# Attention stage of a grid-LSTM, attention and feed-forward kernel: the place of one transposition, and the shape of one product

## The chip, the cores and the metric

The kernel runs on one core of a Trainium2 chip. The metric is the time of one execution on the device in microseconds (us), as the median of several runs. The engines are TensorE (PE, with its weight loads shown apart as PEld), VectorE (DVE), ScalarE (ACT), GpSimd (POOL) and SyncE (SP, which here issues DMAs). Each has its own queue of instructions and works it off in the order in which the kernel was written; they wait for one another by semaphores.

## The reference

The input x is 16 images of 64 x 64 cells with 128 channels, float32. Three layers follow each other:

```
x = x + grid_lstm(group_norm(x))             # 16 x 64 x 64 x 128
t = tokens(x)                                # 16 x 4096 x 128
n = layer_norm(t)
t = t + n + nystrom_attention(layer_norm(n)) # 8 heads of 16, 64 landmarks, plus a convolution of v over 33 rows
n = layer_norm(t)
t = t + sigmoid_recurrence(batch_norm(n @ W.T))
```

The change is in the attention. With q, k, v the projections of the normalised rows, q_l and k_l the means over 64 rows each (landmarks), it computes softmax(q k_l') pinv(softmax(q_l k_l')) (softmax(q_l k') v) + conv(v), multiplies by w_out, and adds. The last part of the attention stage also makes the next layer's input: the layer norm of the sum, turned, and its product with W ("feed"), which is written to memory for the recurrence.

## The kernel before

The attention stage cuts each image into Q = 8 groups of 512 rows. A group passes through three stages that are an image (8 steps) apart, and several groups are in flight. The Python function `step(s)` writes the instructions of one step; it is used for s = 15 to 127, with `first_step` and `second_step` ahead of it and `last_step` behind. In one step, `new` (group s) is projected to keys, values and queries; `mid` (group s - 8) has its weights softmax(q_l k') formed and multiplied with v; and the groups around s - 16 end: `first` is compared with the landmarks and softened (the exponents of the next step's `attend`), `cur` is attended, convolved and divided, `third` goes through w_out and is added to the stream, `fourth` is measured, `fifth` is normalised (tile z), turned, and fed through W. `after` is group s + 1: its rows (tile xh, loaded two steps before) are turned by four transposes of TensorE so that the next step can project them. Nothing is rearranged by a scheduler: the order in the queues of PE, DVE, ACT and POOL is the order of the calls in `step`.

PSUM has eight banks of 512 float32 columns, used by name: `bank0` to `bank5`, and a `pair` of two. A tile in a bank may only be written when all readers of the tile before it in that bank are done. The uses that matter here, in one step, in order:

- bank 0: keys, then the first of four score tiles of `greatest` (L1028), reduced on DVE by `keep_greatest` (L1032) in the order 3, 2, 1, 0; then the first tile of `soften` (L1170, L1172), read by ACT in `softened` (L1177).
- bank 1: values, a tile of `greatest`, the turned stream of `turn_output` (L960, tile z, copied by ACT to zT, L975), a tile of `soften`.
- bank 2: a tile of `greatest`, the turned maxima of `turn_top` (L1159, copied by ACT to topT, L1163), the reciprocals r of `divide` (L1195, read on DVE in L1197), a tile of `soften`.
- bank 3: a tile of `greatest`, the product with w_out (L1212, read on DVE in `keep_sum`, L1216), the feed (L1244, copied by ACT to fx, L1248), a tile of `soften`.
- banks 4 and 5: `weigh`, then the two tiles of `attend` (L1184), transposed on DVE in `divide` (L1193, tile t); then bank 4 takes the turned rows of `turn_rows` (L960, tile xh, copied by ACT to xT, L968), and bank 5 takes `attend_values` (L1080).
- the pair: `weigh`, then `convolve` (L1107), then `compare` (L1135).

TensorE's order in a step is: `compare`, keys, values, queries (L979), `greatest`, `weigh` (L1058, L1064), w_out, `turn_top`, `turn_output`, `attend`, `convolve`, feed, `turn_rows`, `attend_values`, `soften`. The array can be used whole (128*128) or in tiles; keys, values and queries are written as four tiles of 128 rows by 32 columns by the helper `product(..., apart)` (except in the first step of an image), `attend` and `convolve` use 64*32, `weigh`, `soften` and `compare` use 32*128, and w_out, the transposes and the feed use the whole array. A float32 product appears in the trace as two matmuls, a transpose as one.

ACT's order around the change is: four exponentials of `weights` (L1073), zT, topT, fx, xT, a part of `carry` (L948), the four exponentials of `softened`, another `carry`, keys (L987), values (L997).

Of the kernel before, what the change touches and what calls it, by code (L numbers as in the profile page):

```python
# [845 lines left out]
def attention(nc, tc, t1, gamma, beta, wqkv, ident, mhalf, fixed, xp, rows, qm, km, pinvT, vd, t2, wx, wx_stats, out, ahead):  # L846
# [20 lines left out]
    with ExitStack() as ctx:  # L867
# [10 lines left out]
        def banks(*ks):  # L878
            return [bank(k, [P, GC]) for k in ks]
# [4 lines left out]
        bands, wo, bo, wfT, ones, ones_b, minus, ident_b, split, tops, gs = fixed  # L884
# [71 lines left out]
        def turn(a, k):  # L956

            p = bank(k, [P, C, P])
            for c in range(C):
                nc.tensor.transpose(p[:, c, :], a[:, c, :], ident)  # L960
            return p.rearrange("p c n -> p (c n)")

        def turn_rows(gr, k=4):
            gr.px = turn(gr.xh, k)

        def keep_rows(gr):
            gr.xT = wk.tile([P, GC], F32, tag="xT", name="at_xT", bufs=2)
            nc.scalar.activation(gr.xT, gr.px, AF.Identity, bias=beta, scale=gamma)  # L968
# [4 lines left out]
        def keep_output(gr):  # L973
            gr.zT = wk.tile([P, GC], F32, tag="zT", name="at_zT")
            nc.scalar.copy(gr.zT, gr.pz)  # L975

        def product(out, lhsT, rhs, apart):
            for r in map(quarter, range(NP)) if apart else (slice(0, P),):
                nc.tensor.matmul(out[r], lhsT[:, r], rhs, start=True, stop=True)  # L979

        def project_keys(gr, p=None, apart=False):
            gr.pk = banks(0)[0] if p is None else p
            product(gr.pk, wqkv[:, P : 2 * P], gr.xT, apart)

        def keep_keys(gr):
            gr.KT = kv.tile([P, GC], F32, tag="KT", name="at_KT")
            nc.scalar.copy(gr.KT, gr.pk)  # L987

        def project_values(gr, p=None, apart=False):
            gr.pv = banks(1)[0] if p is None else p  # L990
            for c in range(C):
                cs = slice(c * P, (c + 1) * P)
                product(gr.pv[:, cs], gr.xT[:, cs], wqkv[:, 2 * P : 3 * P], apart)
# [7 lines left out]
        def project_queries(gr, apart=False):  # L1001
            (gr.pq,) = banks(5)
            product(gr.pq, wqkv[:, 0:P], gr.xT, apart)
# [44 lines left out]
        def sums(im):  # L1048
            im.sums = sm.tile([P, P], F32, tag="sums", name="at_sums")
            im.total = wk.tile([P, NP, P], F32, tag="total", name="at_total", bufs=2)  # L1050
# [24 lines left out]
        def attend_values(gr, k=5):  # L1075

            p = bank(k, [P, P])
            for c in range(C):
                for n in range(NP):
                    nc.tensor.matmul(  # L1080
                        p[quarter(n)], gr.V[:, c, quarter(n)], gr.e[:, n, c, :],
                        start=(c == 0), stop=(c == C - 1), skip_group_check=True,
                    )
            gr.p = p

        def keep_values(gr):
            im, p = gr.im, gr.p
            if gr.g == 0:
                nc.vector.tensor_copy(im.sums, p)
            else:  # L1090
                nc.vector.tensor_tensor(im.sums, p, im.sums, ALU.add)
# [37 lines left out]
        def compare(gr):  # L1129

            gr.both = pair()
            gr.s = (*banks(4, 5), gr.both[:, 0], gr.both[:, 1])
            for c in range(C):
                for n in range(NP):
                    nc.tensor.matmul(  # L1135
                        gr.s[n][:, c * P : (c + 1) * P], gr.QT[quarter(n), c * P : (c + 1) * P],
                        gr.im.km[quarter(n)], start=True, stop=True,
                    )

        def topmost(gr):  # L1140
            gr.mx = sm.tile([P, NP, C, 2], F32, tag="cmx", name="at_cmx")
            for s, n, k in ((gr.s[1], 1, 1), (gr.both.rearrange("p n x -> p (n x)"), 2, 2), (gr.s[0], 0, 1)):
                nc.vector.tensor_reduce(  # L1143
                    gr.mx[:, n : n + k].rearrange("p n c j -> p (n c j)"), s.rearrange("p (x m) -> p x m", m=M), AX.X, ALU.max
                )
# [28 lines left out]
        def softened(gr):  # L1174
            gr.eT = wk.tile([P, NP, GC], F32, tag="eT", name="at_eT")
            for n in range(NP):
                nc.scalar.activation(gr.eT[:, n], gr.s[n], AF.Exp)  # L1177
# [42 lines left out]
        def measure(gr, cs=range(C)):  # L1220
            if 0 in cs:
                gr.mu = sm.tile([P, C, 2], F32, tag="mu", name="at_mu")
            for c in cs:
                st = sm.tile([P, 6], F32, tag="st", name="at_st")
                nc.vector.bn_stats(st, gr.u[:, c, :])
                nc.vector.bn_aggr(gr.mu[:, c, :], st)
# [12 lines left out]
                    gr.z[:, c, :], gr.u[:, c, :], AF.Identity, bias=gr.nb[:, c : c + 1], scale=gr.r3[:, c : c + 1]  # L1239
                )  # L1240

        def feed(gr, k=3):
            (gr.pf,) = banks(k)
            nc.tensor.matmul(gr.pf, wfT, gr.zT, start=True, stop=True)  # L1244

        def keep_feed(gr):
            gr.fx = fx = wk.tile([P, GC], F32, tag="fx", name="at_fx")
# [3 lines left out]
        def measure_feed(gr):  # L1251
            nc.vector.bn_stats(wx_stats[:, gr.im.b * Q + gr.g, :], gr.fx)
# [3 lines left out]
        def group(s):  # L1256
            b, g = divmod(s, Q)
            return images[b].groups[g] if b in images else None
# [141 lines left out]
        def step(s):  # L1400
            b, q = divmod(s, Q)
            new, after, mid, was = group(s), group(s + 1), group(s - Q), group(s - Q - 1)
            first, cur, third, fourth, fifth, sixth = (group(s - 2 * Q + d) for d in (1, 0, -1, -2, -3, -4))
            start = q == 0
            if first:
                compare(first)
            if cur:
                softened(cur)
            project_keys(new, apart=not start)
            if start:  # L1410
                sums(mid.im)
            project_values(new, apart=not start)
            if s == 2 * Q - 1:
                attend_values(was, 3)
                keep_values(was)
            if first:
                topmost(first)
            if sixth:
                measure_feed(sixth)
            if fourth:  # L1420
                measure(fourth, (0,))
            keep_keys(new)
            keep_projected(new)
            project_queries(new, apart=not start)
            if start and was:
                gather(was.im)
            if fourth:
                measure(fourth, (1,))
            keep_queries(new)
            if start:  # L1430
                turn_split(mid.im)
            if fifth:
                normalise(fifth)
            greatest(new)
            if first:
                carry_factors(first)
                carry(first, 2, nc.gpsimd)
            weigh(mid)
            keep_greatest(new)
            if first:  # L1440
                part_top(first)
            if third:
                output(third)
            weights(mid)
            if first:
                carry(first, 3, nc.gpsimd)
            if start and was:
                spread_values(was.im)
            if first:
                turn_top(first)  # L1450
            if fifth:
                turn_output(fifth)
                keep_output(fifth)
            if third:
                keep_sum(third)
            if fourth:
                measure(fourth, (2, 3))
            if cur:
                attend(cur)
            if first:  # L1460
                keep_top(first)
            add_weights(mid, (3, 1, 0), mid.g == 0)
            if fourth:
                factors(fourth)
            add_weights(mid, (2,))
            if q == Q - 1:
                shift(new.im)
            if cur:
                convolve(cur, pair())
                divide(cur)  # L1470
            if fifth:
                feed(fifth)
            if after:
                turn_rows(after)
            if fifth:
                keep_feed(fifth)
            if after:
                keep_rows(after)
            if first:
                carry(first, 0, nc.scalar)  # L1480
            attend_values(mid)
            if cur:
                add_convolved(cur)
            keep_values(mid)
            if first:
                soften(first)
                carry(first, 1, nc.scalar)
                carry_bias(first)
            if cur:
                turn_attended(cur)  # L1490
            fetch(s)
# [345 lines left out]
```

## Time and profile before

| what | value |
|---|---|
| median of 3 runs | 3635.04 us (3631.91 to 3635.63) |
| the profiled execution | 3638.43 us, span 3636.9 us |
| PE busy in the span | 3499.9 us (96%) |
| DVE, ACT, POOL busy | 2982.8 (82%), 2499.9 (69%), 2489.2 (68%) |
| mean granted TensorE clock | 0.99 |
| first and last `attend` in `step` | 1734.5 and 3121.2 us |

How to read it: a row of a timeline has the start in us from the start of the span, the duration from there to the end of the last of its instructions, the engine, the line of the kernel, the operation, its output and input tiles, the shape, and the number of instructions. Rows of matmuls overlap: a matmul's record lasts until its last result has left the array, while the next one is already streaming, so the time that a group holds the array is read from its start to the start of the next group. In brackets at the end of a row is the time for which the engine stood idle before it and what it is taken to have waited for.

### The profile page before, as it was taken

How to read it: one execution, taken by the hardware profiler on the slowest of the kernel's cores; microseconds unless marked ns; L12 is line 12 of the kernel's file. 1: busy time of each engine (PE TensorE's matmuls, PEld its weight loads, DVE VectorE, ACT ScalarE, POOL GpSimd, SP SyncE). 2: the span in 40 equal slices, each digit the busy share in tenths (PEclk: the TensorE clock that was granted, in tenths of full speed). 3: DMA queues.
4: the chain of work that ended last, by engine and by line, in shares of the span. 5: the costliest groups of instructions: out<-in, count | busy, mean ns of one | idle time of the engine just before them, and what ended most of it. 6: DMA issues, size and time to landing. Idle time of an engine off the chain costs nothing. (4 is left out here: it accounts for less than half of the span.)

```text
span 3636.9 us, 106193 instructions
## 1 busy us (share of the span) xinstructions
PE 3499.9 (96%) x40438; PEld 2343.7 (64%) x40438; DVE 2982.8 (82%) x7005; ACT 2499.9 (69%) x5126; POOL 2489.2 (68%) x3843
## 2 busy tenths in 40 slices
PE   7899999999999998999999999999999999997988
PEld 5666665545567666985666666666666666654777
DVE  8699999998889887544888888888888888888665
ACT  0466556656667665445788888888888888876787
POOL 1577877777788885434777777777777777785223
PEclk9999999999999999999999999999999999999999
DMA  9223232333333321023677777777777777667799
GB/s 339 83 76 80 80 86 80 84 84 83 85 88 86 81 76 38 4 63 92 147 185 187 164 162 163 166 167 163 164 166 166 165 164 168 157 143 187 201 273 182
DMA packets 834210, 484.50 MB, mean 133 GB/s; under 512 B 304672, under 2 KB 800672, under 8 KB 833696
## 3 DMA queue, kind: packets, MB, share of 16 engines
q1 hardware_dynamic: 814026, 442.55, 47.8%
q0 software_dynamic: 17728, 34.61, 5.3%
q8 instruction: 322, 5.28, 0.6%
q14 instruction: 192, 1.57, 0.1%
q10 hardware_dynamic: 1942, 0.50, 0.1%
HBM read 239.21 MB, written 238.29 MB: 131 GB/s over the span
## 5 line engine op out<-in xcount | busy, mean ns | idle before, releaser
L1100 POOL TENSOR_TENSOR at_total<-at_total,at_e 128x512 f32<-128x512 f32 x472 | 603.1, 1278 | 228.3 <-ACT at_e L1073 208.6
L290 ACT ACTIVATE ls_g<-ls_z,ls_b 128x304 f32<-128x304 f32 (+26 forms) x950 | 494.0, 545 | 225.0 <-PE ls_z L288 192.7
L283 PE MATMUL ls_z<-ls_xn,ls_w 128*128 128x432 f32 (+28 forms) x1700 | 586.1, 492 | 1.5 <-POOL ls_xn L275 1.2
L283 PEld LDWEIGHTS ls_z<-ls_xn,ls_w 128*128 128x128 f32 x1700 | 309.6, 191 | 189.4 <-issue 98.1
L288 PE MATMUL ls_z<-ls_hsum,ls_u 128*128 128x304 f32 (+26 forms) x1140 | 369.7, 461 | 0.0
L1032 DVE TENSOR_REDUCE at_mxq<-at_bank 128x1 f32<-128x512 f32 x512 | 314.9, 677 | 53.0 <-PE at_bank L1028 53.0
L323 POOL TENSOR_TENSOR ls_tt<-ls_ve,mhalf 128x8 f32<-128x8 f32 (+2 forms) x190 | 312.7, 1646 | 19.8 <-DVE ls_ve L322 4.2
L288 PEld LDWEIGHTS ls_z<-ls_hsum,ls_u 128*128 128x128 f32 x1140 | 211.6, 194 | 128.6 <-issue 78.4
L1177 ACT ACTIVATE at_eT<-at_bank 128x512 f32<-128x512 f32 x512 | 264.5, 604 | 42.1 <-PE at_bank L1172 41.5
L406 ACT ACTIVATE ls_g<-ls_cell 128x304 f32<-128x304 f32 (+26 forms) x190 | 93.2, 491 | 268.1 <-DVE ls_cell L405 267.8
L288 PE MATMUL ls_z<-ls_h,ls_u 128*128 128x304 f32 (+26 forms) x760 | 256.2, 460 | 12.3 <-DVE ls_h L410 12.3
L402 POOL TENSOR_TENSOR ls_g<-ls_g,ls_cell 128x304 f32<-128x304 f32 (+26 forms) x190 | 180.1, 948 | 127.7 <-ACT ls_g L290 113.0
L340 ACT ACTIVATE ls_tt<-ls_tt,ls_nb 128x128 f32<-128x128 f32 (+9 forms) x632 | 261.0, 478 | 5.6 <-POOL ls_tt L323 5.0
L979 PE MATMUL at_bank<-at_xT,wqkv 128*32 128x512 f32 (+1 forms) x1684 | 262.8, 602 | 2.0 <-DVE at_cmx L1143 1.1
L275 POOL TENSOR_TENSOR ls_xn<-ls_xn,grstd 128x272 f32<-128x272 f32 (+40 forms) x186 | 209.9, 1129 | 76.2 <-DVE ls_xn L270 71.2
L1143 DVE TENSOR_REDUCE at_cmx<-at_bank 128x8 f32<-128x512 f32 x256 | 175.6, 686 | 103.8 <-PE at_pair L1135 102.1
L1248 ACT COPY at_fx<-at_bank 128x512 f32<-128x512 f32 x128 | 133.7, 1044 | 142.9 <-PE at_bank L1244 138.3
L1619 DVE SCALAR_TENSOR_TENSOR rc_y<-rc_w,rc_scale,rc_z 128x256 f32<-128x256 f32 x344 | 154.6, 481 | 86.3 <-PE rc_z L1606 84.5
L1238 ACT ACTIVATE at_z<-at_u,at_nb,at_r 128x128 f32<-128x128 f32 x512 | 209.6, 484 | 4.6 <-POOL at_nb L1233 4.5
L288 PEld LDWEIGHTS ls_z<-ls_h,ls_u 128*128 128x128 f32 x760 | 141.9, 193 | 107.8 <-issue 53.2
L1600 POOL DMA_DIRECT2D out_dram<-rc_tt x64 | 77.4, 1209 | 168.4 <-ACT rc_tt L1597 145.0
L1193 DVE STREAM_TRANSPOSE at_t<-at_bank 128x512 f32<-128x512 f32 x256 | 167.9, 695 | 25.3 <-PE at_bank L1184 25.2
(281 smaller groups left out, 9683.8 us busy)
## 6 DMA issues: line engine op xcount, KB each, us to landing
at_win<-vd SPq DMA_DIRECT2D x256, 256.0 KB
t<-ls_tt SPq DMA_DIRECT2D x392, 130.0 KB
at_T<-t SPq DMA_DIRECT2D x128, 264.0 KB
gs_xb<-in_x_dram SPq DMA_DIRECT2D x64, 512.0 KB
at_xh<-t SPq DMA_DIRECT2D x128, 256.0 KB
vd<-at_v SPq DMA_DIRECT2D x128, 256.0 KB
t<-at_u SPq DMA_DIRECT2D x128, 256.0 KB
out_dram<-at_u SPq DMA_DIRECT2D x128, 256.0 KB
```

The source lines that it names most:

```text
L275: eng.tensor_tensor(a, a, norm(v, grstd), ALU.mult)
L283: nc.tensor.matmul(v.z[g][:, : v.total], wt[g], v.xn[:, : v.total], start=True, stop=True)
L288: nc.tensor.matmul(view(v, v.first.z[g]), ut[g], hin, start=False, stop=True, skip_group_check=True)
L290: nc.scalar.activation(a[:, : v.cols], z, AF.Tanh if g == 4 else AF.Sigmoid, bias=bt[g])
L323: nc.gpsimd.tensor_tensor(v.tt[:, 0:k, F + 2 : F + 4], ve[:, :, :k].rearrange("p r k -> p k r"), mhalf[:, : 2 * k].rearrange("p (k r) -> p ...
L340: nc.scalar.activation(v.tt[:q, k, F + 4 :], v.tt[:q, k, 0:F], AF.Identity, bias=v.nb[:q, k : k + 1], scale=v.tt[:q, k, F + 3 : F + 4],)
L402: nc.gpsimd.tensor_mul(v.a[1], v.a[1], v.cl)
L979: nc.tensor.matmul(out[r], lhsT[:, r], rhs, start=True, stop=True)
L1032: nc.vector.tensor_reduce(gr.im.mxq[:, n : n + 1, gr.g], gr.s[n], AX.X, ALU.max)
L1100: eng.tensor_tensor(total, total, e[:, :, c, :], ALU.add)
L1177: nc.scalar.activation(gr.eT[:, n], gr.s[n], AF.Exp)
L1238: nc.scalar.activation(gr.z[:, c, :], gr.u[:, c, :], AF.Identity, bias=gr.nb[:, c : c + 1], scale=gr.r3[:, c : c + 1])
```

## The change

In `step`, the four transposes of the next group's rows (`turn_rows`) and their copy (`keep_rows`) are called right behind `turn_output` and `keep_output`, ahead of `keep_sum` and `attend`, and the rows are turned into bank 0 in place of bank 4. The product of the feed is written by the helper `product` as four products of 32 output channels each (128 rows by 32 columns of the array, 512 streamed columns), all into the same bank 3. `last_step` calls `feed` without the new argument, and the other steps are as before.

```diff
-        def feed(gr, k=3):
+        def feed(gr, k=3, apart=False):
             (gr.pf,) = banks(k)
-            nc.tensor.matmul(gr.pf, wfT, gr.zT, start=True, stop=True)
+            product(gr.pf, wfT, gr.zT, apart)
...
             if fifth:
                 turn_output(fifth)
                 keep_output(fifth)
+            if after:
+                turn_rows(after, 0)
+                keep_rows(after)
             if third:
                 keep_sum(third)
...
             if fifth:
-                feed(fifth)
-            if after:
-                turn_rows(after)
-            if fifth:
+                feed(fifth, apart=True)
                 keep_feed(fifth)
-            if after:
-                keep_rows(after)
             if first:
                 carry(first, 0, nc.scalar)
             attend_values(mid)
```

The order on TensorE becomes: ..., `turn_top`, `turn_output`, `turn_rows`, `attend`, `convolve`, feed, `attend_values`, `soften`. The order on ACT becomes: ..., zT, xT, topT, fx, `carry`, `softened`.

## The prediction

> **What bounds the kernel now.** I read the page first. TensorE (PE) is busy for 96% of the span, yet matmul records overlap, so that figure alone does not make it the limit. The table by windows places the change: lines 1454 to 1476 belong to `step`, whose `attend` groups stand between 1734 and 3122 us, and there PE has no hole.
>
> ```profile
> 2200.00:2450.00 250.00, 249.05 (x4246) 162.37 (x4242) 219.25 (x472) 205.59 (x409) 194.48 (x343) 1.00 0.72 165
> 2204.28:2216.97 12.69, 12.69 (x223) 8.15 (x223) 11.32 (x25) 10.65 (x22) 10.10 (x17) 1.00 0.73 169
> 2426.28:2439.12 12.84, 12.84 (x223) 8.26 (x223) 11.34 (x25) 10.69 (x22) 10.11 (x17) 1.00 0.73 167
> ```
>
> The columns are the stretch, its length, the busy time of PE, PEld, VectorE (DVE), ScalarE (ACT) and POOL, the granted clock (1.00), the DMA share and GB/s. PE is busy for 249 of 250 us. The second row is one step, from one start of `attend` (L1184) to the next: 12.69 us, which nearly all steps with this body take to a hundredth (the first step of an image takes 15.80). The third row is one that took 12.84; it will be my price list. Next I read the timeline of one step, engine by engine.
>
> ```profile
> 2203.74 0.60 PE L960 MATMUL at_bank<-ident,at_z 128*128 128x128 f32 x4
> 2204.28 1.09 PE L1184 MATMUL at_bank<-at_eT,at_g 64*32 64x512 f32 x16
> 2205.16 0.64 PE L1107 MATMUL at_pair<-at_win,bands 64*32 64x256 f32 x16
> 2205.73 1.12 PE L1244 MATMUL at_bank<-at_zT,at_wfT 128*128 128x512 f32 x2
> 2206.69 0.60 PE L960 MATMUL at_bank<-ident,at_xh 128*128 128x128 f32 x4
> 2207.22 1.08 PE L1080 MATMUL at_bank<-at_e,at_v 128*32 128x128 f32 x32
> 2208.24 0.40 PE L1170 MATMUL at_bank<-at_topT,at_minus 32*128 32x512 bf16 x4
> 2208.46 1.03 PE L1172 MATMUL at_bank<-at_QT,km 32*128 32x512 f32 x8
> ```
>
> Start to start tells what each group holds of the array: turn of the stream .54, attend .88, convolve .57, feed .96, turn of the rows .53, attend_values 1.02, the first products of `soften` .22. Nothing on PE waits for another engine here, but one group comes close. `soften` writes banks 0 to 3; bank 2 holds `r`, the reciprocals of `divide`, until VectorE has read them in L1197, and VectorE gets there by a chain that begins when `attend` has filled bank 4:
>
> ```profile
> 2203.38 0.68 DVE L1032 TENSOR_REDUCE at_mxq<-at_bank 128x1 f32<-128x512 f32 x1
> 2205.46 1.31 DVE L1193 STREAM_TRANSPOSE at_t<-at_bank 128x512 f32<-128x512 f32 x2
> 2206.88 0.36 DVE L1195 RECIPROCAL at_bank<-at_t 128x32 f32<-128x32 f32 x1
> 2207.27 0.69 DVE L1197 TENSOR_TENSOR at_m<-at_t,at_bank 128x512 f32<-128x512 f32 x1
> ```
>
> In times from the start of `attend` (2204.28): at_t begins at 1.18, right after bank 4 is complete (1.16 in the records of semaphores), at_t ends at 2.49, L1197 ends at 3.68. `soften` starts at 3.96. A wait of PE for VectorE costs about .05 from the end of one record to the start of the other (shown below), so bank 2 is free for PE at 3.73, and the slack is **.23 us a step**. That is the number on which the case turns: two chains run from `attend` to `soften`, PE's own of 3.96 and VectorE's of 3.73.
>
> The slower step shows what a late L1197 costs:
>
> ```profile
> 2429.23 0.36 DVE L1195 RECIPROCAL at_bank<-at_t 128x32 f32<-128x32 f32 x1 [0.46 <-DVE at_t L1193]
> 2429.62 0.69 DVE L1197 TENSOR_TENSOR at_m<-at_t,at_bank 128x512 f32<-128x512 f32 x1
> 2430.23 0.52 PE L1170 MATMUL at_bank<-at_topT,at_minus 32*128 32x512 bf16 x4
> 2430.46 1.15 PE L1172 MATMUL at_bank<-at_QT,km 32*128 32x512 f32 x8
> ```
>
> Here L1195 started .35 late (why, the profile does not say), L1197 ended at 2430.31, and the third product of L1170 started (one by one in the trace) at 2430.36 instead of 2430.24: .12 late, and the step became .15 longer. Four steps of this kind are in the trace, with 12.84 or 12.85. So nothing behind `soften` gives the time back: a late bank 2 goes into the period in full.
>
> **The change part by part** (times still from the start of `attend`).
>
> *Feed as four tiles.* 2 matmuls of 128*128 become 8 of 128*32. The same form is `project_keys` (L979, 8 matmuls over 512 columns), which holds the array for .88 from its start to that of the values behind it, against .96 for the feed: -.08, the weight load that stands before the second 128*128 product. Its successor, attend_values, is also 128*32.
>
> The Trainium skill (TensorEngine Tiling (Array Packing), When to Use Tiling) advises column tiles where the stationary side has at most 64 columns; this one has 128, so by that rule the split gains nothing; the rows of L979 and L1244 give .08. The same page (Key Properties) says that changing the tiling mode drains the array, which the change does one time less in each step; by that rule alone the change would be a gain.
>
> *One change of tile shape less.* Each shows as a gap beyond the streaming time: z turn to attend .09, convolve to feed .14, rows to attend_values .09, attend_values to soften .12. The shape 128*128 between feed and attend_values goes: -.09, and about -.03 for the first weights of attend_values. How long 64*32 to 128*32 takes isn't shown; the four gaps bound it at .09 and .14. It makes no difference below, because PE will be waiting.
>
> *The turn of the rows moves* by four transposes, .109 each start to start: +.44 between the z turn and `attend`, -.44 behind the feed. What PE must do in a whole step thus falls by .08 + .09 + .03 = **.20**.
>
> *A new wait.* Bank 0 is read by `keep_greatest`, last of its four reductions (order 3, 2, 1, 0): the L1032 row ends at 2204.06, so at -.22, and PE knows at -.17. The rows' first transpose could start at -.09, and its weights are fetched as the last z transpose starts, at -.20. So the wait costs 0 to .07, the latter if the whole weight load (.14) follows it; nothing below 0, because the transposes can't come before the z turn. I take .03, the delay of the fetch. Behind it on PE stand attend, convolve, feed, and all that follows.
>
> *ACT.* `keep_rows` (.76) moves ahead of keep_top, keep_feed and the first `carry`. ACT is idle for 1.17 us in front of keep_feed, and that covers it: zT is still ready at 2205.24, as the feed needs; topT would end at about 2206.5, and who waits for it needs it later (L1195 at about 2207.3, soften). Without that cover it would be .76 a step. xT comes earlier, and nobody waits for it. SP: no DMA moves; the load of xh was issued two steps before in either order. POOL and the order on DVE stay.
>
> *Where the .44 lands.* `attend` starts .44 to .51 later, I take .47. VectorE's chain starts from bank 4 and has no slack in it: in the shown step its previous instruction had ended when bank 4 was filled. So it moves as a whole, 3.73 behind `attend`. PE's chain behind `attend` shrinks by .64, from 3.96 to 3.32, and must wait: for bank 5 (at_t ends at 2.49, PE at 2.54, attend_values instead of 2.31), which lets soften's first product go at 3.56; for bank 3, which keep_feed reads (the feed's record would end at 2.49, where it now ends at 2.57; the copy L1248 begins .04 later and takes 1.04; so PE has the bank at 3.62); and for bank 2 at 3.73, the latest of the three. The step is then 12.69 + .47 - .23 = 12.93, **+.24**. With a wait of 0 it is +.21. The slow step adds about .03 for the staggered products, which gives +.27 at the other side.
>
> The body runs with `cur` and `after` in 111 steps (16 to 126; in the longer first steps of the images, too, at_t starts as bank 4 fills and L1197 ends at 3.68): 111 x .24 = **+27 us**, and 23 to 30 by the bounds. The profiled execution took 3638.4 (span 3636.9 and 1.5 around it), so it would become 3665; the median of the runs shown is 3.4 lower, and the forecast for a median is **3661**.
>
> **The rivals.**
>
> *The three waits do not bind, PE remains the limit* (the other side). Then the step is .20 shorter: 111 x .20 = 22 us, 3613. It decides from the point where L1197 ends earlier than 3.27 behind `attend`. For it: PE has no hole now, and PE's work falls. Against it: at_t alone (1.18 + 1.31) and the two rows behind it with the short gaps between give 3.68 in all but the four late steps.
>
> *Bank 2 does not bind but bank 3 and bank 5 do*: if PE's window of waiting instructions let the products of banks 0, 1 and 3 and their second products go past the one for bank 2. Then soften goes on at 3.62, .34 earlier than now: .44 or .47 less .34 is +.10 to +.13 a step, 12 us, 3647. For it: in the slow step .12 of delay is shorter than L1195's .35, but that is the slack of .23; the two products for banks 0 and 1 did go ahead and the step was still longer, which speaks against it.
>
> *The wait for bank 0 is dearer*: .07 for the fetch plus the .03 of the stagger, or a reduction that comes later when VectorE is pushed: +.34 a step, 38 us, 3673. VectorE still has .92 of idle time before topmost, which speaks against a further push.
>
> *The turn does not follow at once*, because the wait for bank 0 holds PE so long that no shape change is saved: that is the same place at a higher price, and it is in the chance of the last one. That all of it cancels (gain .20 against a wait of .20) would need a chain of VectorE shorter by .24.
>
> **How the numbers follow.** What a measurement of this kernel can tell from no change is about 0.2%, 7 us. Bank 2 late, 3656 to 3668: .77. Bank 0 dearer, about 3673: .08. Banks 3 and 5 alone, 3647: .06. Cancelled, within 7 us: .04. PE still the limit, 3613: .05. So faster .05, same .04, slower .91. The range goes from the milder rival's lower end (111 x .09, 3645) to the dearer one's 3674.
>
> **What the profile after would show.** `attend` to `attend` 12.90 to 12.96 us. L1170 starts 3.56 behind `attend` with a third product at 3.73, .05 behind the end of L1197. The feed holds the array for .88. Attend_values waits for at_t. VectorE's idle time in front of at_t is about .45. The .92 in front of topmost falls to about .7. ACT's 1.17 in front of keep_feed falls to about .8 (less .76 for xT, plus .35 for the later feed). I am wrong if steps of 12.5 appear, or if L1197 has ended when attend_values ends; and the size is wrong if the L960 rows of xh start more than .2 behind the last of z.

## The result, and the profile after

| | before | after |
|---|---|---|
| median of 6 runs each | 3635.82 us (3631.91 to 3640.54) | 3664.14 us (3660.06 to 3668.29) |
| the profiled execution, its span | 3638.43, 3636.9 | 3660.06, 3658.6 |
| first `attend` of `step` to that of s = 127 | 1450.2 us | 1477.4 us |
| a regular step, `attend` to `attend` | 12.693 us | 12.927 us |
| the first step of an image | 15.80 us | 16.02 us |

The change makes the kernel slower: 28.3 us, ratio 1.0076, 95% interval 1.0064 to 1.0089. The loss lies where it was expected. Over the 111 steps with the new body the two profiled executions differ by 27.2 us; what follows is 1.0 us shorter (451.2 for 452.2), and the stages ahead, which the change does not touch, happened to be 4.5 us shorter in that execution (1730.0 for 1734.5), so that the spans differ by 21.7 only. The `attend` of s = 127 stands at 3184.7 us in the kernel before; 3121.2 and 3122, given above for the last one in `step`, belong to one five steps earlier. The count of 111 steps isn't touched by that.

One step in the table by windows, of the kernel after (stretch, length, busy time of PE, PEld, DVE, ACT, POOL, granted clock, DMA share, GB/s):

```profile
2234.64:2247.56 12.92, 12.89 (x229) 8.06 (x229) 11.32 (x25) 10.69 (x23) 10.14 (x17) 1.00 0.69 166
```

The clock is full, and VectorE, ScalarE and GpSimd work as many us as in the step of before; the step is merely longer. PE still looks busy: a record lasts until its last result has left the array, and so covers most of a wait that follows. In the timeline below the feed's row ends at 2237.15, .03 before `attend_values` starts, though the feed holds the array for .88 only, until 2236.97 (a hold that e9 below shows without a wait behind it). So this column can't tell a wait from work. Start times can. The timeline of PE in that step, after:

```profile
2233.66 0.61 PE L960 MATMUL at_bank<-ident,at_z 128*128 128x128 f32 x4
2234.11 0.60 PE L960 MATMUL at_bank<-ident,at_xh 128*128 128x128 f32 x4
2234.64 1.09 PE L1184 MATMUL at_bank<-at_eT,at_g 64*32 64x512 f32 x16
...
2236.09 1.06 PE L979 MATMUL at_bank<-at_zT,at_wfT 128*32 128x512 f32 x8
2237.18 1.08 PE L1080 MATMUL at_bank<-at_e,at_v 128*32 128x128 f32 x32
2238.20 0.56 PE L1170 MATMUL at_bank<-at_topT,at_minus 32*128 32x512 bf16 x4
2238.42 1.19 PE L1172 MATMUL at_bank<-at_QT,km 32*128 32x512 f32 x8
2239.34 0.40 PE L1135 MATMUL at_bank<-km,at_QT 32*128 32x128 f32 x2
...
2240.46 0.64 PE L979 MATMUL at_bank<-at_xT,wqkv 128*32 128x512 f32 x4
```

Measured from the start of `attend`: the feed at 1.45, `attend_values` at 2.55, `soften` at 3.56 with its third product (one by one in the trace) at 3.73, `compare` at 4.70, the next keys at 5.82. The L1170 row has grown to .56, the sign of four products that no longer start together. The chain of VectorE in the same step, after (in brackets: idle before the row, and what ended it):

```profile
2235.82 1.31 DVE L1193 STREAM_TRANSPOSE at_t<-at_bank 128x512 f32<-128x512 f32 x2 [0.45 <-PE at_bank L1184]
2237.23 0.36 DVE L1195 RECIPROCAL at_bank<-at_t 128x32 f32<-128x32 f32 x1
2237.63 0.69 DVE L1197 TENSOR_TENSOR at_m<-at_t,at_bank 128x512 f32<-128x512 f32 x1
2238.42 0.69 DVE L1203 TENSOR_TENSOR at_m<-at_pair,at_m 128x512 f32<-128x512 f32 x1
2239.03 0.28 DVE L1091 TENSOR_TENSOR at_sums<-at_bank,at_sums 128x128 f32<-128x128 f32 x1
...
2240.62 0.69 DVE L1143 TENSOR_REDUCE at_cmx<-at_bank 128x8 f32<-128x512 f32 x1 [0.70 <-PE at_pair L1135]
```

It is the chain of before, moved as a whole: at_t begins 1.18 after `attend`, L1197 ends 3.68 after it, and VectorE now idles .45 until `attend` has filled bank 4. PE's third product of `soften` starts .05 behind the end of L1197, as the prediction has it.

The last rows show what the prediction did not look at. `compare` (L1135, the first call of the next `step`) overwrites bank 5, out of which `keep_values` (L1091) reads. L1091 ends at 4.675 behind `attend`; the second product of `compare`, the one for bank 5, starts at 4.728. That is a **second stop on the same chain**: a second place where PE waits for a bank that VectorE reads. The same two rows before, where `attend` stood at 2204.28:

```profile
2208.67 0.28 DVE L1091 TENSOR_TENSOR at_sums<-at_bank,at_sums 128x128 f32<-128x128 f32 x1
2209.32 0.27 PE L1135 MATMUL at_bank<-km,at_QT 32*128 32x128 f32 x2
```

There `compare` stood at 5.04 and bank 5 was clear for PE at 4.73, a slack of .31. The table of waits after hardly shows this stop: between 1800 and 3100 us it has L1135 waiting for L1091 twice, .4 us in all, and puts PE's waiting down to `attend_values` (L1080, for at_t, 97 times, 91.2 us), the first of the groups that wait for this chain.

### The profile page after: what moved, and what is told of

The parts are those of the page before. It is cut to its first block, busy times and chain, and to the rows that moved or that the text cites. A ratio compares the mean times of both kernels' runs of the same rounds, so it can differ in the third digit from the quotient of the medians.

```text
span 3658.6 us, 107525 instructions
## 1 busy us (share of the span) xinstructions
PE 3512.7 (96%) x41092; PEld 2327.9 (64%) x41092; DVE 2984.2 (82%) x7005; ACT 2505.7 (68%) x5126; POOL 2495.1 (68%) x3843
```

## The experiments

Differences and ratios are against the kernel before, in the same session and on the same chip. "Step" is the median of a regular step, `attend` to `attend`.

**The two parts apart.** e1 is the kernel after with the feed whole again; e2 is the kernel before with the feed alone as four tiles.

```diff
 e1, against after:
-                feed(fifth, apart=True)
+                feed(fifth)
 e2, against before:
-                feed(fifth)
+                feed(fifth, apart=True)
```

> The rows are turned early into bank 0 as in the change, but the feed stays one product of the whole array. Theory (attend comes .44 us later, and soften waits for bank 2, which VectorE reads 3.73 us behind attend): the feed then ends .08 later, attend_values waits for bank 5 until 2.54 anyway, and soften's third product still goes at 3.73. The step stays at 12.93 us, the time within 3 us of the changed kernel, about 28 us over the kernel before. Rival (the loss comes from the four tiles): the step falls to 12.5 to 12.7 us, and the time to that of the kernel before or under it.

Measured: 3661.58, +29.0 us, ratio 1.0082 [1.0068, 1.0096], step 12.927. The whole loss is in the moved rows, and the tiles give nothing beside it, as expected.

> The feed as four tiles of 128x32, the rows turned where they were, behind it and into bank 4. Theory: attend keeps its place, so VectorE's chain keeps its slack of .23 us and TensorE alone decides: -.08 us for the feed, and a change of shape more, from 128x32 back to the whole array for the rows, .09 to .14 and up to .11 for the first weight load. The step becomes 12.70 to 12.86 us, the time 1 to 18 us over the kernel before, 10 most likely. Rival (the four tiles alone explain the loss): the step 12.93, +28 us. Rival (they are a plain gain): 12.61, -9 us.

Measured: 3642.75, +10.2 us, ratio 1.0025 [1.0015, 1.0035], step 12.787 (+.094). The timeline of PE in e2:

```profile
2232.53 1.06 PE L979 MATMUL at_bank<-at_zT,at_wfT 128*32 128x512 f32 x8
2233.53 0.66 PE L960 MATMUL at_bank<-ident,at_xh 128*128 128x128 f32 x4
2234.12 0.97 PE L1080 MATMUL at_bank<-at_e,at_v 128*32 128x128 f32 x28
```

The tiled feed holds the array for 1.00 up to the rows where the whole one held it for .96, and the rows hold it for .59 instead of .53, since their second transpose follows the first by .16 and not by .11. The change of shape from the feed to the rows is new, and it costs more than the .08 that the tiles save. Without the move, the tiles are a loss. In the kernel after, another 128*32 group follows them; what they are worth there, e6 and e8 show.

**Where does r lie?** If bank 2 is what binds, r in another place frees `soften`. e3 keeps r in SBUF:

```diff
-            r = bank(k, [P, 2, NB])
+            r = bank(k, [P, 2, NB]) if k else sm.tile([P, 2, NB], F32, tag="r", name="at_r2")
```

> The changed kernel with the reciprocals of divide written to SBUF in place of bank 2, so that soften no longer waits for VectorE's reading of them. Theory: bank 2 was only the last of three; bank 3, which the copy of the feed reads until 3.63 us behind attend, now binds at 3.68, and the first product still goes at 3.56. The step falls by .04 to .09 us, to 12.84 to 12.89, the time by 5 to 10 us to some 20 us over the kernel before. Rival (bank 2 is all of it): the step falls to 12.49 to 12.55, the time to 13 to 20 us under the kernel before. Rival (bank 2 does not matter): 12.93 as before.

Measured: 3755.08, +122.5 us, ratio 1.0340 [1.0326, 1.0354], step 13.92. No expectation had that. The timelines of VectorE and GpSimd in e3:

```profile
2224.83 4.00 POOL L1100 TENSOR_TENSOR at_total<-at_total,at_e 128x512 f32<-128x512 f32 x3 [2.66 <-ACT at_e L1073]
...
2227.62 1.76 DVE L1197 TENSOR_TENSOR at_m<-at_t,at_r 128x512 f32<-128x512 f32 x1
...
2300.30 0.72 DVE L1197 TENSOR_TENSOR at_m<-at_t,at_r 128x512 f32<-128x512 f32 x1
```

With both inputs in SBUF, L1197 takes 1.76 instead of .69: it started at 2227.62, GpSimd's three additions ended at 2228.83, and it ended .55 after them. In the last row, from the first step of an image, where no such addition runs beside it, it takes .72. GpSimd's next instruction (L52) takes .54 instead of .22. So r is in PSUM for a reason, and the run tests neither the bank nor the theory. The Trainium skill (SBUF — State Buffer, section on SBUF's two separate sides) says that VectorE and GpSimd share a pair of ports, that an operation of VectorE with two inputs in SBUF needs it, and that whoever comes second is blocked for the whole instruction of the other; the 1.76 beside the .72 agrees, and e4 below shows it in both directions.

**All three waits of the prediction taken away at once**, first with r in SBUF still:

```diff
 e4: r as in e3, and
-            product(gr.pf, wfT, gr.zT, apart)
+            product(gr.pf, wfT, gr.zT.rearrange("p (c l) -> p l c", l=STEPS) if apart else gr.zT, apart)
...
-            attend_values(mid)
+            attend_values(mid, 4)
```

The feed's columns are streamed in the order in which they are stored, so that the copy to fx is contiguous and bank 3 comes free earlier, and `attend_values` goes to bank 4.

> The changed kernel with all three waits of soften and attend_values taken away: reciprocals in SBUF; attend_values into bank 4, which VectorE has read .6 us before bank 5; and the feed streams its columns in the order in which the result is stored, so that the copy of the feed is contiguous (some .62 us as zT's copy, where it took 1.04). Theory: TensorE is then the limit again, attend_values follows the feed at once, soften starts 3.35 us behind attend; the step is 12.49 us and the time about 22 us under the kernel before, 50 under the changed one. If the strided stream slows the feed, the step grows by that and the feed's row shows it. Rival (the loss lies elsewhere, in the early transposes or in ACT's order): the step stays above 12.69.

Measured: 3774.72, +142.1 us, ratio 1.0391 [1.0377, 1.0406], step 13.94. The cost is a new one, in the timeline of PE in e4:

```profile
2231.78 2.52 PE L979 MATMUL at_bank<-at_zT,at_wfT 128*32 128x512 f32 x8
2233.85 1.32 PE L1080 MATMUL at_bank<-at_e,at_v 128*32 128x128 f32 x32
```

A stream that steps 128 bytes from column to column makes the feed hold the array for 2.07 us instead of .88, and `attend_values` behind it takes 1.26 instead of 1.02. L1197 is slow in a third of the steps only. In 54 of 103 it started within .1 us of an addition of GpSimd and took .69, and that addition took 1.85 instead of 1.28; in 32 it took 1.84 and the addition 1.3. So either engine can come first, and the other waits. A step of the first kind (the second addition starts with L1197):

```profile
2275.29 0.69 DVE L1197 TENSOR_TENSOR at_m<-at_t,at_r 128x512 f32<-128x512 f32 x1
2273.87 3.28 POOL L1100 TENSOR_TENSOR at_total<-at_total,at_e 128x512 f32<-128x512 f32 x2
```

Both runs failed as tests, and the next ones avoid these costs.

**r in another PSUM bank**, and nothing else:

```diff
 e5:
-                divide(cur)
+                divide(cur, 4)
```

> The changed kernel with the reciprocals of divide in bank 4, which VectorE itself has just read, in place of bank 2: in PSUM as before, so that their reader keeps its .69 us, but soften does not wait for them. Theory: of the three waits bank 2 is the last at 3.73 us behind attend, and bank 3, which the copy of the feed reads until 3.63, the next at 3.69. The step falls only by .03 to .07 us, to 12.86 to 12.90, the time by 3 to 8 us from the changed kernel's, to some 22 us over the kernel before. Rival (bank 2 is all of it): the step falls to 12.49 to 12.73, the time to the level of the kernel before or under it.

Measured: 3668.50, +33.5 us, ratio 1.0093 [1.0079, 1.0107], step 12.928. The product for bank 2 now went with the first two and only that for bank 3 came .13 later, at 3.69, so that `compare` could start at 4.65 instead of 4.70. Yet its second product, for bank 5, stands at 4.73 as before, and the step is as long as before this edit. Against the prediction's account, in which bank 2 is "the latest of the three", this is a miss: something later holds PE to the same time.

**All three waits away without the side effects**: r in bank 5, `attend_values` in bank 4, and zT written by ACT in the order of storage (1.06 us instead of .62, ACT has room), so that both the feed's stream and the copy to fx (.59 instead of 1.04) are contiguous.

```diff
 e6:
-            nc.scalar.copy(gr.zT, gr.pz)
+                nc.scalar.copy(gr.zT.rearrange("p (l c) -> p c l", l=STEPS), gr.pz.rearrange("p (c l) -> p c l", l=STEPS))
...
-            nc.scalar.copy(fx.rearrange("p (l c) -> p c l", l=STEPS), gr.pf.rearrange("p (c l) -> p c l", l=STEPS))
+                nc.scalar.copy(fx, gr.pf)
...
-                keep_output(fifth)
+                keep_output(fifth, True)
...
-                divide(cur)
+                divide(cur, 5)
...
-            attend_values(mid)
+            attend_values(mid, 4)
```

> The changed kernel with all three waits taken away, without the strided stream and without reciprocals in SBUF: attend_values into bank 4, the reciprocals into bank 5, and the stream's copy zT written in the order in which the feed is stored, so that the feed streams it contiguously and its copy fx is contiguous too (some .6 us, where it took 1.04; the strided write moves to zT's copy, which is ready at about .95 where the feed starts at 1.45). Theory: TensorE is the limit again, attend_values follows the feed at once, soften starts 3.35 us behind attend; the step is 12.49 to 12.52, the time 20 to 22 us under the kernel before and some 50 under the changed one. Rival (another wait stands close behind the three, such as VectorE's for the end of compare or topT's for soften): the step stays between 12.55 and 12.93, and the row that waits shows which.

Measured: 3669.04, +34.0 us, ratio 1.0097 [1.0082, 1.0113], step 12.934 instead of 12.49. The timeline of PE in e6, one step (line numbers 4 higher than in after), then that of VectorE:

```profile
2229.93 0.40 PE L1174 MATMUL at_bank<-at_topT,at_minus 32*128 32x512 bf16 x4
...
2231.33 0.38 PE L1139 MATMUL at_bank<-km,at_QT 32*128 32x128 f32 x2 [0.15 <-DVE at_sums L1095]
```

```profile
2231.00 0.28 DVE L1095 TENSOR_TENSOR at_sums<-at_bank,at_sums 128x128 f32<-128x128 f32 x1
```

`attend` stands at 2226.61. `soften` goes at 3.32, unwaited, all four products together (.40 again), as the prediction's chain of PE without waits has it. Then `compare` stands until 4.72, .05 after L1095 has ended at 4.67. The table of waits of e6 (1800 to 3100 us) has it 86 times:

```profile
PEld at_bank L1139 <- DVE at_sums L1095: 85.2, 86, 1.4
```

This is where the theory "bank 2 sets the step" had to be widened: bank 2 holds `soften`, and the bank of `attend_values` holds `compare`, both on VectorE's chain from `attend`, and either stop gives the same step.

**Two variants of e6** meet the same stop at `compare`.

```diff
 e7, against e6:
-                divide(cur, 5)
+                divide(cur)
 e8, against e6:
-                feed(fifth, apart=True)
+                feed(fifth)
```

> As the run with all three waits taken away, but the reciprocals stay in bank 2: only the waits for banks 3 and 5 go. Theory (bank 2 alone is enough for the whole loss): soften's first product starts at 3.35 behind attend, its third still at 3.73; the step is 12.89 to 12.93, the time within 5 us of the changed kernel's. Rival (banks 3 and 5 carry a part of the loss): the step falls below 12.85.

Measured: 3669.60, +34.6 us, ratio 1.0092 [1.0077, 1.0108], step 12.933. The step is at the upper end of what was expected, but e6 without bank 2 has the same, so the time tells nothing apart. The timeline of PE in e7 does (`attend` at 2229.27):

```profile
2232.59 0.80 PE L1174 MATMUL at_bank<-at_topT,at_minus 32*128 32x512 bf16 x4
```

The first product of `soften` goes at 3.32, the third not before 3.73, and the last one of the group at 4.40. That is where it goes in the kernel after (4.40), in which banks 5 and 3 are late too. So bank 2, without the other two, puts the end of `soften` where it is.

> As the run with all three waits taken away, but with the feed as one product of the whole array. Theory: TensorE is the limit, so the terms that the four tiles were priced at now show in full: .08 for the feed's second weight load, .09 for the change of shape to attend_values, .03 for its first weights; soften starts at 3.52 to 3.55, the step is 12.66 to 12.72, the time within 4 us of the kernel before. Rival (the four tiles are worth nothing): the step is that of the run with all waits taken away, about 12.5.

Measured: 3666.62, +31.6 us, ratio 1.0084 [1.0070, 1.0098], step 12.933 instead of 12.69. `soften` goes at 3.52 where e6 has 3.32: the .20 of the feed's shape (`attend_values` starts .17 later and holds the array .02 longer) is there in full, and hidden behind the wait of `compare`.

**The chain of VectorE cut short.** Leaving out `add_convolved` (L1203), the link between L1197 and `keep_values`, moves the release of `compare` forward by .8 and leaves that of bank 2 where it is. The convolution's product is still formed. e9 is e6 without it (neither stop), e10 is the kernel after without it (the stop of `soften` alone):

```diff
-            if cur:
-                add_convolved(cur)
```

> The three waits of soften and attend_values taken away as before, and VectorE's addition of the convolved values left out in step (so the convolution is missing from these groups' results). In the earlier run without the three waits the step stayed at 12.93, and compare, not soften, stood: its first product came at 4.73 us behind attend, .05 behind the end of keep_values on VectorE, though soften had left the array at 4.42. New theory: compare overwrites bank 4 or 5 and the pair, which VectorE empties at the end of the same chain (keep_values at 4.68, the convolution's addition at 4.47); bank 2 is an earlier stop of it. Without the addition keep_values ends at about 4.06 and TensorE is the limit: the step falls to 12.49 to 12.53, the time to 17 to 22 us under the kernel before. Rival (something else in front of compare): the step stays above 12.7.

> The changed kernel, with the reciprocals in bank 2, bank 5 and the copy of the feed as they are, and only VectorE's addition of the convolved values left out in step (so the convolution is missing). Compare can then go at 4.43. If bank 2 alone costs as much as was forecast, soften's third product still goes at 3.73, its second half ends at 4.81, and the step is 12.88 to 12.92, the time 19 to 27 us over the kernel before. Rival (only compare's wait cost anything): the step falls below 12.75, the time to within 6 us of the kernel before.

Measured in one session: e9 3613.52, -21.2 us, ratio 0.9939 [0.9926, 0.9953], step 12.498; e10 3658.37, +23.7 us, ratio 1.0068 [1.0054, 1.0082], step 12.900. The timeline of PE in e9 (`attend` at 2231.04), then that of e10 (`attend` at 2235.15):

```profile
2234.36 0.40 PE L1174 MATMUL at_bank<-at_topT,at_minus 32*128 32x512 bf16 x4
...
2235.45 0.27 PE L1139 MATMUL at_bank<-km,at_QT 32*128 32x128 f32 x2
...
2236.44 0.70 PE L983 MATMUL at_bank<-at_xT,wqkv 128*128 128x512 f32 x1
```

```profile
2238.71 0.56 PE L1170 MATMUL at_bank<-at_topT,at_minus 32*128 32x512 bf16 x4
...
2239.85 0.28 PE L1135 MATMUL at_bank<-km,at_QT 32*128 32x128 f32 x2
```

In e9 every row of PE follows its predecessor: `soften` at 3.32, `compare` at 4.41, keys at 5.40. In e10 `soften` is at 3.56 and .56 long again, its third product at 3.73, and `compare`, for which VectorE is long done, stands at 4.70 because of `soften` alone. So the stop of `soften`, which by e7 is set by bank 2, costs 12.900 - 12.693 = .207 a step, and PE without either stop would have gained 12.693 - 12.498 = .195. With e6 (the stop of `compare` alone, 12.934) and the kernel after (both, 12.927) all four cases are measured.

**Can the second stop be moved with all the work done?** e11 is e6 with the sum of `keep_values` taken from VectorE: a copy out of PSUM by ACT, and the addition on GpSimd. e12 is e11 with the last group of each image added on VectorE as it was, and `compare`'s products for the pair issued first.

```diff
 e11, against e6:
-            keep_values(mid)
+            keep_values_aside(mid)
...
+                nc.scalar.copy(part, p)
+                nc.gpsimd.tensor_tensor(im.sums, part, im.sums, ALU.add)
 e12, against e11:
+            elif gr.g == Q - 1:
+                nc.vector.tensor_tensor(im.sums, p, im.sums, ALU.add)
...
-                for n in range(NP):
+                for n in (2, 3, 0, 1):
```

> A whole kernel: the three waits taken away, and keep_values taken from VectorE: ACT copies the 128x128 product out of bank 4 (some .3 us, in its idle time before soften's exponentials) and GpSimd adds it to the sums (.4 us or so, in its idle time). Then compare waits only for the convolution's addition, which ends at 4.47 us behind attend (4.52 at TensorE), where soften leaves the array at 4.42. The step falls to 12.55 to 12.65, the time 5 to 15 us under the kernel before and 30 to 40 under the changed one. Rival (ACT's copy delays the exponentials, or GpSimd is pushed into VectorE's way): the step stays at 12.7 or more.

Measured: 3696.35, +61.7 us, ratio 1.0164 [1.0150, 1.0177]. The regular step fell to 12.722, less far than to the 12.55 to 12.65 expected, since `compare`'s products for the pair wait until 4.52 and the group then holds the array for 1.21. The first steps of the images took 20.04 in the median instead of 16.02. The timelines of PE and GpSimd at the start of an image in e11 show why this is so:

```profile
2158.25 0.45 POOL L1104 TENSOR_TENSOR at_sums<-at_part,at_sums 128x128 f32<-128x128 f32 x1
2158.75 0.33 PE L1129 MATMUL at_bank<-ident,at_sums 128*128 128x128 f32 x1 [1.28 <-POOL at_sums L1104]
```

`gather` (L1129) needs the sums of the whole image, and the last addition sat in GpSimd's queue behind `shift`. PE waited 1.28 us for it, and for some 7 us after such a wait the granted clock stood at 0.5.

> A whole kernel. The run that took keep_values from VectorE came out slower for two reasons that its trace shows: compare's third product waited for the pair until 4.53 us behind attend while its first two had gone at 4.40, and the products then ran staggered, 1.21 us in place of .99; and at each new image TensorE waited 1.3 us for GpSimd's last addition to the sums, after which the granted clock stood at one half for some 7 us. Here the last group of each image is added on VectorE again, and compare issues the two products into the pair first, so that all four start together. Theory: compare starts at 4.53 and takes .99, the step is 12.58 to 12.64 (12.93 in the last step of an image), no half clock at the images' starts, and the time is 5 to 11 us under the kernel before. Rival (the stagger comes from somewhere else): the step stays at 12.72 and the time at or a little over that of the kernel before.

Measured: 3653.59, +14.4 us, ratio 1.0039 [1.0025, 1.0053], step 12.742, first steps 16.02, no half clock. All four products of `compare` now start together, 4.53 behind `attend`, released by `add_convolved`. What is missing to 12.50 is .12 of waiting (4.53 instead of e9's 4.41) and .11 in `compare` itself, in the timeline of PE in e12:

```profile
2239.97 0.38 PE L1150 MATMUL at_pair<-km,at_QT 32*128 32x128 f32 x2
...
2240.19 0.28 PE L1150 MATMUL at_pair<-km,at_QT 32*128 32x128 f32 x2
```

The next pair of products starts .21 later, where e9 has .11. In the trace the first weight load starts together with the first product, at 4.53; in e9 it starts at 3.98, while `soften` still streams. So the wait costs its own length and then the load. That is better than the kernel after and worse than the kernel before. No kernel here that does all the work beats the kernel before.

## Why the prediction was right, and what it missed

- **The amount and the sign** hold: 28.3 us measured, 27 forecast (23 to 30 by the bounds); a step of 12.927 where 12.93 was forecast.
- **The move**: `attend` starts .441 later behind the z turn (.976 for .535). The wait for bank 0, taken at .03 within 0 to .07, measured 0: xh's first transpose follows the last of z by .109, like any other, in 91 of 95 regular steps (by .15 in four).
- **VectorE's chain moves as a whole**: right (idle .45 in front of at_t, .70 in front of topmost, as forecast; .92 in front of keep_feed where .8 was said).
- **The work of PE falls by .20**: e9 measures it, .195. Its terms show in e6 and e8, which differ by the feed's shape alone: the tiled feed holds the array for .88, and whole it puts `attend_values` .17 later, .08 + .09 as forecast, and `soften` .02 more, where .03 was forecast.
- **`attend_values` waits for bank 5 until 2.54, `soften` goes at 3.56 with a third product at 3.73**: measured 2.55, 3.56, 3.73.
- **"Bank 2 at 3.73, the latest of the three"** is true of the three (bank 3 came at 3.69 in e5, where 3.62 was forecast), and incomplete. The stop of `soften` costs .207 (e10), which is .441 - .23 = .21 by the prediction's own sum with a bank-0 wait of nothing. The remaining .027 of the .234 is `compare`, behind `keep_values`, a term that the prediction put at nothing without looking at it. In e10 and in the kernel after, `compare` starts at the same 4.70, but after it holds the array for 1.12 and not for 1.10, its second product waiting. Where the stop of `soften` is gone or earlier, `compare` alone costs .235 to .241 (e5, e6): in e6, .441 for the rows, less .31 for its start (4.73 instead of 5.04), plus .11 because it holds the array for 1.10 instead of .99. So the two stops don't add, the later one decides, and here they lie .03 apart.
- **Luck**: the forecast of .24 had the .03 from bank 0, where it was not, in place of the .03 at `compare`. That the two are alike is luck: with the bank-0 wait of nothing that was measured, the prediction's own sum gives .21, its lower bound. It is luck too that the stop it missed lies only .03 behind the one it had.
- **The rivals**: that PE remains the limit had the right price, 3613 forecast and 3613.5 in e9, though not in the way it was put. Its condition, L1197 ending before 3.27, did not occur and was not tried; taking the banks of `soften` out of L1197's way is not enough (e5, e6), `keep_values` has to end earlier too (e9). Banks 3 and 5 alone did not occur. The dearer bank 0 did not either.
- **The four late steps of before** (three of 12.84, one of 12.80), from which bank 2's price was read, fit both stops alike, since a late L1195 delays both. In the one that the prediction shows, L1091 ends 5.03 behind `attend` and the second product of `compare` starts at 5.08, so the second stop could have been read there. Why L1195 was late in them stays open, as does whether the .23 and the .31 could be had back by starting VectorE's chain earlier, which was not tried.

## What to carry to other kernels

When a chain of one engine is pushed back, list every release that it still owes to the other engine, in the code of the next iteration too, each with its slack: the loss is the largest excess, not the sum, and taking away one stop alone gives nothing while another lies as late. PE's busy share shows none of this; start times counted from a common event do. A run that leaves out a link of the chain tells what the engine itself would allow, which no rearrangement of banks did.

## What the runs showed of the hardware

- A VectorE product of two SBUF operands took 1.76 us beside GpSimd's additions and .72 without them (e3); with one operand in PSUM it took .69 beside the same additions. Where it came first by a hundredth, it took .69 and GpSimd's addition 1.85 instead of 1.28 (e4).
- A float32 stream with a step of 128 bytes held the array for 2.07 us where the contiguous one takes .88 (e4, with four tiles). The Trainium skill (Advanced Engine Details and Errata, SBUF Cachelines) speaks of lines of 16 bytes and of a penalty where each access falls into another line; the direction agrees, the size is this run's.
- The wait in front of `compare`, a group of short matmuls, cost more than its length: the group took 1.10 instead of .99 with all four products released at once (e6, e12), its first weight load starting with the first product and not ahead of it.
- A wait of 1.28 us of PE in the first step of an image was followed by 6.8 us at a granted clock of 0.5 (e11, from 2159.8 us).
